# Group norm's scale and bias moved from the weights into the norm, the norm of later images moved to ScalarE, and a new order of the first loads and projections

## The chip, the cores and the metric

The kernel runs on one core of a Trainium2 chip. The metric is the device time of one execution in microseconds (us). Several executions were timed, and one was profiled.

## The reference, cut to what matters

Two layers on x of shape (8, 32, 32, 512), everything in float32. The change touches the first layer alone: a group norm with 32 groups of 16 channels, a projection to q, k and v, attention with 8 heads of 64, an output projection and a residual.

```python
xg = x.reshape(b, h * w, NUM_GROUPS, c // NUM_GROUPS)
mu = jnp.mean(xg, axis=(1, 3), keepdims=True)
var = jnp.var(xg, axis=(1, 3), keepdims=True)
xn = (xg - mu) * jax.lax.rsqrt(var + EPS)
x_norm = xn.reshape(b, h, w, c) * gn_scale + gn_bias
...
qkv = x_norm @ w_qkv + b_qkv
q, k, v = jnp.split(qkv, 3, axis=-1)
...
weight = jnp.einsum('bhld,bhsd->bhls', q * scale, k * scale)
weight = jax.nn.softmax(weight, axis=-1)
out = jnp.einsum('bhls,bhsd->bhld', weight, v)
...
out = out @ w_out + b_out
x = x_flat + out
```

`scale` is 1/8, so q and k together carry 1/64, which the kernel puts on q alone (`1.0 / HD`). The second layer is a deformable attention with a layer norm, a depthwise convolution, a bilinear gather, an attention over 256 sampled keys, and an MLP.

## The kernel before

An image has 1024 tokens, kept as 8 tiles of 128 tokens by 512 channels. The first layer works through the images one after the other, each in 32 steps of its main loop (line 728 on): 4 pairs of heads times 8 tiles of 128 queries. One such step calls `att.push` (line 749), which makes the scores of two heads on TensorE (`sc`, 128 x 1024 each), their row maxima on VectorE (`nmax`), the exponentials on ScalarE (`e`), and a 32 x 32 block transpose of them on VectorE (`sq`). After every second step the SP queue issues 16 DMAs (`moved`, line 204) that finish the transpose (`et`), and a few steps later TensorE multiplies `et` by the values (`av`). The scores of two heads fill the two `sc` buffers, so the scores of a step wait for the exponentials of the step before. There are two `e` buffers.

All other work of the layer is placed between these by hand. `at(place, step)` (line 347) puts a step on a list, and `run_due` issues what is due: between the exponentials and the transposes of step n all places under n + 0.8, after the transposes all under n + 1. `InOrder` (line 42) keeps every engine in this program order.

- `norm_steps` (line 440) loads and norms an image: `turn` (eight times) transposes a tile of x on TensorE into `xT` (channels on partitions, 512 tokens a block, two blocks an image, three buffers) with a copy by ScalarE, and asks POOL for the next tile of x; `two_tiles` takes statistics on VectorE; `gather`, `means` and `deviations` make the mean `mu` and the reciprocal deviation `rs` of every channel's group, with two small matmuls, and a power on POOL; `norm` applies them to the block, four VectorE instructions of 128 x 512 each. For an image after the first these stand in the previous image's loop, at the places in `norm_places` (line 718), counted from its start.
- `qkv_steps` (line 504) has six projections for one pair of heads: keys, queries and values for each of the two blocks (`rows` and `values`). For the first pair of the first image all six are issued before the loop (line 725, the place -1); for the first pair of a later image they stand at 26.3 to 31.3 of the image before (`pair_places[0]`).
- The group norm's scale is multiplied into `wqkv` in front of the loop (lines 419 to 421), as is q's 1/64. Its bias is multiplied by the weights with `add_cols` (line 415, 48 matmuls with one column) and added to `bqkv`. `add_row` (line 416) takes the values' part of that through `wout` and adds it to the row `bout`.
- In front of the loop POOL's queue loads four tiles of the first x (line 400, four buffers), and SP's queue loads the vectors, the three thirds of `wqkv`, `bout`, `wout` and two rows (lines 402 to 411). The last four tiles of x are asked for by `turn`, as buffers come free.

Of the kernel before, what the change touches and what calls it, by code (L numbers as in the profile page):

```python
# [9 lines left out]
F32 = mybir.dt.float32  # L10
I32 = mybir.dt.int32
AF = mybir.ActivationFunctionType
ALU = mybir.AluOpType
# [4 lines left out]
P = 128  # L18
B = 8
H = W = 32  # L20
S = H * W
C = 512
NC = C // P
NT = S // P
QB = 512
# [3 lines left out]
HD = 64  # L29
# [201 lines left out]
def attention_then_deformable_attention(  # L231
# [30 lines left out]
    nc = tc.nc  # L262
# [28 lines left out]
    def load_cols(pool, v, name):  # L291
        t = pool.tile([P, v.shape[0] // P], F32, tag=name, name=name)
        with nc.allow_non_contiguous_dma(reason="a vector onto partitions"):
            nc.sync.dma_start(t, v.rearrange("(c p) -> p c", p=P))
        return t
# [6 lines left out]
    def add_cols(dst, w, vec, on_scalar=False):  # L302

        n = dst.shape[1]
        ps = mm_tile()
        for o in range(n):
            for c in range(NC):
                nc.tensor.matmul(
                    ps[:, o : o + 1],
                    lhsT=w[:, c, ts(o, P)],  # L310
                    rhs=vec[:, c : c + 1],
                    start=(c == 0),
                    stop=(c == NC - 1),
                )
        if on_scalar:
            for o in range(n):
                col = dst[:, o : o + 1]
                nc.scalar.activation(col, ps[:, o : o + 1], AF.Identity, bias=col)
        else:
            nc.vector.tensor_tensor(dst, ps[:, 0:n], dst, ALU.add)  # L320
# [26 lines left out]
    def at(place, step):  # L347
        due.append((place, len(due), step))
# [37 lines left out]
    with ExitStack() as l0:  # L386
# [3 lines left out]
        nc = InOrder(tc)  # L390
# [2 lines left out]
        xs = {}  # L393

        def load_x(b, t):
            if b < B:
                xs[b, t] = work.tile([P, C], F32, tag="x", name="x", bufs=NX)
                nc.gpsimd.dma_start(xs[b, t], x_tok[b][ts(t, P), :])

        for t in range(NX):  # L400
            load_x(0, t)
        gsc = load_cols(wp, gn_scale, "gsc")
        gbi = load_cols(wp, gn_bias, "gbi")
        bqkv = load_cols(wp, b_qkv, "bqkv")
        wqkv = wp.tile([P, NC, 3 * C], F32, tag="wqkv", name="wqkv")
        for i in range(3):
            nc.sync.dma_start(wqkv[:, :, ts(i, C)], by_chunk(w_qkv)[:, :, ts(i, C)])
        bout = load_row(wp, b_out, "bout")
        wout = load_w(wp, w_out, "wout")
# [1 line left out]
        lnb_row = load_row(wp, ln_b, "lnb_row")  # L411

        add_cols(bqkv, wqkv, gbi)
        add_row(work, bout, wout, bqkv[:, 2 * NC : 3 * NC])


        for c in range(NC):
            nc.vector.tensor_scalar(wqkv[:, c, :], wqkv[:, c, :], gsc[:, c : c + 1], None, ALU.mult)  # L420
            nc.vector.tensor_scalar(wqkv[:, c, 0:C], wqkv[:, c, 0:C], 1.0 / HD, None, ALU.mult)
        nc.vector.tensor_scalar(bqkv[:, 0:NC], bqkv[:, 0:NC], 1.0 / HD, None, ALU.mult)


# [15 lines left out]
        def norm_steps(b, start, places):  # L440

            room = {}

            def turn(t):
                blk, i = divmod(t, NQT)
                if i == 0:
                    xTs[b, blk] = work.tile([P, NC, QB], F32, tag="xT", name="xT", bufs=NX_T)
                if t == 0:
                    room["stats"] = work.tile([P, NC, NT // 2, 6], F32, tag="stats", name="stats")
                ps = mm_tile()  # L450
                for c in range(NC):
                    nc.tensor.transpose(ps[:, ts(c, P)], xs[b, t][:, ts(c, P)], ident)
                nc.scalar.copy(xTs[b, blk][:, :, ts(i, P)], ps.rearrange("p (c q) -> p c q", q=P))
                load_x(b + (t + NX) // NT, (t + NX) % NT)

            def two_tiles(i):
                blk, half = divmod(i, NQT // 2)
                for c in range(NC):
                    nc.vector.bn_stats(
                        room["stats"][:, c, i, :], xTs[b, blk][:, c, ts(half, 2 * P)]  # L460
                    )


            def gather():
                mv = room["mv"] = work.tile([P, NC, 2], F32, tag="mv", name="mv")
                stats = room["stats"]
                for c in range(NC):
                    nc.vector.bn_aggr(mv[:, c, :], stats[:, c, :, :].rearrange("p s f -> p (s f)"))

            def means():  # L470
                mv = room["mv"]
                ps = mm_tile()
                nc.tensor.matmul(ps[:, 0:NC], lhsT=gmat, rhs=mv[:, :, 0], start=True, stop=True)
                mu = room["mu"] = work.tile([P, NC], F32, tag="mu", name="mu")
                nc.vector.tensor_copy(mu, ps[:, 0:NC])
                dev = room["dev"] = work.tile([P, NC], F32, tag="dev", name="dev")
                nc.vector.tensor_tensor(dev, mv[:, :, 0], mu, ALU.subtract)
                nc.vector.tensor_tensor(dev, dev, dev, ALU.mult)
                nc.vector.tensor_tensor(dev, dev, mv[:, :, 1], ALU.add)

            def deviations():
                ps = mm_tile()
                nc.tensor.matmul(ps[:, 0:NC], lhsT=gmat, rhs=room["dev"], start=True, stop=True)
                room["rs"] = work.tile([P, NC], F32, tag="rs", name="rs")
                rstd(room["rs"], ps[:, 0:NC], 1e-6)

            def norm(blk):
                xT, mu, rs = xTs[b, blk], room["mu"], room["rs"]
                for c in range(NC):
                    nc.vector.tensor_scalar(  # L490
                        xT[:, c, :], xT[:, c, :], mu[:, c : c + 1], rs[:, c : c + 1],
                        ALU.subtract, ALU.mult,
                    )

            steps = [
                *(lambda t=t: turn(t) for t in range(NT)),
                *(lambda i=i: two_tiles(i) for i in range(NT // 2)),
                gather, means, deviations,
                *(lambda blk=blk: norm(blk) for blk in range(NQB)),
            ]  # L500
            for place, what in zip(places, steps):
                at(start + place, what)

        def qkv_steps(b, hp, places):

            room = qkv[b, hp] = {}

            def rows(name, w0, bias, blk):
                if blk == 0:
                    room[name] = work.tile([P, S], F32, tag=name, name=name)  # L510
                xT = xTs[b, blk]
                ps = project(lambda c: wqkv[:, c, ds(w0, P)], lambda c: xT[:, c, :])
                out = room[name][:, ts(blk, QB)]
                if name == "k":
                    out = room[name].rearrange("p (s j q) -> p s j q", s=NSQ, q=SQ)
                    out, ps = out[:, :, ts(blk, NQT), :], att.by_blocks(ps)
                nc.scalar.activation(out, ps, AF.Identity, bias=bias)

            def values(t0):
                if t0 == 0:  # L520
                    room["v"] = work.tile([P, NT, P], F32, tag="v", name="v")
                xT = xTs[b, t0 // NQT]
                ps = mm_tile()
                for i in range(4):
                    for c in range(NC):
                        nc.tensor.matmul(
                            ps[:, ts(i, P)],
                            lhsT=xT[:, c, ts(i, P)],
                            rhs=wqkv[:, c, ds(2 * C + hp * P, P)],
                            start=(c == 0), stop=(c == NC - 1),  # L530
                        )
                nc.scalar.copy(room["v"][:, t0 : t0 + 4, :], ps.rearrange("p (t o) -> p t o", o=P))

            kb, qb = bqkv[:, NC + hp : NC + hp + 1], bqkv[:, hp : hp + 1]
            steps = [
                step
                for blk in range(NQB)
                for step in (
                    lambda blk=blk: rows("k", C + hp * P, kb, blk),
                    lambda blk=blk: rows("q", hp * P, qb, blk),  # L540
                    lambda blk=blk: values(blk * NQT),
                )
            ]
            for place, s in zip(places, steps):
                at(place, s)
# [73 lines left out]
        def first_conv(n):  # L619
# [98 lines left out]
        norm_places = [  # L718
            *(18.6, 19.6, 20.6, 21.6, 22.4, 22.5, 23.3, 23.4),
            *(20.85, 21.86, 22.86, 23.95),  # L720
            *(24.9, 24.96, 25.25, 25.85, 25.86),
        ]
        out_places = [0.3, 1.3, 4.3, 6.3, 7.3, 8.3, 10.3, 11.3]
        norm_steps(0, -100, norm_places)
        qkv_steps(0, 0, [-1] * 6)
        run_due(0)
        attT = {}
        for b in range(B):
# [487 lines left out]
```

## Time and profile before

| | us |
|---|---|
| median of 3 runs | 3833.03 |
| lowest and highest | 3826.36, 3833.45 |
| the profiled execution | 3831.76 |
| its span, first to last instruction | 3830.1 |
| TensorE busy in the span | 3609.5 (94%) |
| VectorE busy | 2831.4 (74%) |
| ScalarE busy | 1491.3 (39%) |
| GpSimd (POOL) busy | 754.9 (20%) |

The first layer takes the span's first 2100 us or so, the second the rest. Busy time on TensorE is not all work: a group of matmuls in which one waits for another engine still counts between its first and last record. In the profile PE is TensorE's matmul, DVE is VectorE, ACT is ScalarE and SPq the DMA issues of SyncE. L53 is the line of the helper that records every operation, so instructions are told apart by the tiles that they write and read, as in `sc<-k,q`. A float32 matmul of the program shows as two records. Three readings of the start:

```profile
x<-in_x_dram POOLq DMA_DIRECT2D x12, 256.0 KB, 3.4
wqkv<-in_L_conv_w_qkv_dram SPq DMA_DIRECT2D x3, 1024.0 KB, 10.0
...
bqkv<-in_L_conv_b_qkv_dram SPq DMA_DIRECT2D x1, 6.0 KB, 3.8
```

These are DMA issues of the first 60 us: how many, the size of each, and the median time from issue to landing.

### The profile page before, as it was taken

What the parts mean: (1) busy time and instruction counts of PE and PEld (TensorE: products, weight loads), DVE (VectorE), ACT (ScalarE), POOL (GpSimd) and SP (SyncE); (2) the same over time, 40 slices, a digit from 0 to 9 for tenths busy, and PEclk for the clock granted to TensorE, in tenths of its full rate; (3) what the DMA queues carried; (4) which work ended last, traced back from release to release, by engine and by line L of the source; (5) the groups of instructions that cost most, each with busy time, mean ns of one, the idle gap of its engine ahead of it and who ended that gap; (6) DMA issues with size and microseconds to landing.
All of it is one profiled execution on the core that took longest, in us unless ns stands there. A gap on an engine that the chain in (4) does not pass through costs nothing. (4 is left out here: it accounts for less than half of the span.)

```text
span 3830.1 us, 46258 instructions
## 1 busy us (share of the span) xinstructions
PE 3609.5 (94%) x16248; PEld 1889.5 (49%) x16248; DVE 2831.4 (74%) x4305; ACT 1491.3 (39%) x3162; POOL 754.9 (20%) x842
## 2 busy tenths in 40 slices
PE   7999999999999999999998877999999999999997
PEld 4454554545545545455454443454545445454543
DVE  3778677777776877767866659888888888888333
ACT  1443343433434434334354122343434444434443
POOL 1002103012030120210336300212121212121212
PEclk8999999999999999999999988999999999999999
DMA  2666566666665665665755501111111111111100
GB/s 92 163 162 181 157 157 187 162 166 167 163 188 155 164 179 160 172 165 149 206 139 148 171 25 53 47 57 54 56 55 56 55 55 56 55 52 34 61 23 30
DMA packets 235094, 438.23 MB, mean 114 GB/s; under 512 B 49296, under 2 KB 53392, under 8 KB 231920
## 3 DMA queue, kind: packets, MB, share of 16 engines
q1 hardware_dynamic: 211952, 362.04, 34.5%
q0 software_dynamic: 21760, 71.16, 5.9%
q8 instruction: 129, 2.11, 0.2%
q10 hardware_dynamic: 1152, 2.10, 0.1%
q14 instruction: 101, 0.83, 0.1%
HBM read 115.84 MB, written 50.86 MB: 44 GB/s over the span
## 5 line engine op out<-in xcount | busy, mean ns | idle before, releaser
L53 ACT ACTIVATE e<-sc,nmax 128x1024 f32<-128x1024 f32 (+1 forms) x1024 | 805.2, 799 | 951.9 <-DVE nmax L53 950.5
L53 DVE TENSOR_REDUCE nmax<-sc 128x1 f32<-128x1024 f32 (+1 forms) x640 | 753.2, 1218 | 471.6 <-PE sc L53 470.2
L53 DVE SCALAR_TENSOR_TENSOR o<-pad,dww,o 128x256 f32<-128x256 f32 x1344 | 721.8, 537 | 44.1
L53 DVE STREAM_TRANSPOSE sq<-e 128x1024 f32<-128x1024 f32 x512 | 608.6, 1226 | 50.5 <-ACT e L53 48.3
L53 PE MATMUL sc<-k,q 64*128 64x512 f32 x2048 | 537.4, 620 | 16.0 <-ACT e L53 9.1
L53 PE MATMUL av<-et,v 128*64 128x256 f32 x4096 | 502.2, 388 | 16.6 <-DMA et<-sq 9.7
L53 PE MATMUL mm<-xT,wqkv 128*128 128x512 f32 x1024 | 470.7, 603 | 2.1 <-DVE xT L53 2.1
L53 PEld LDWEIGHTS av<-et,v 128*64 128x64 f32 x4096 | 275.5, 137 | 321.0 <-issue 174.2
L53 POOL TENSOR_TENSOR mv<-mv,minus_half 128x1 f32<-128x1 f32 x128 | 74.3, 581 | 1401.8 <-DVE mv L53 1350.7
L53 PEld LDWEIGHTS sc<-k,q 64*128 64x128 f32 x2048 | 185.5, 187 | 285.9 <-issue 225.9
L53 PEld LDWEIGHTS mm<-xT,wqkv 128*128 128x128 f32 x1024 | 185.6, 190 | 225.4 <-issue 222.3
L53 ACT COPY et<-mm 128x512 f32<-128x512 f32 x256 | 141.1, 594 | 317.4 <-PE mm L53 316.8
L53 PE MATMUL mm<-wqkv,xT 128*128 128x128 f32 x2048 | 244.4, 278 | 0.0
L53 PE MATMUL mm<-wm,zT 128*128 128x512 f32 x512 | 241.0, 614 | 2.9 <-ACT zT L53 2.9
L53 PEld LDWEIGHTS mm<-wqkv,xT 128*128 128x128 f32 x2048 | 233.9, 192 | 19.6 <-issue 19.6
L53 PE MATMUL mm<-hat_h,wqq 128*128 128x512 f32 x512 | 236.7, 605 | 0.0
L53 PE MATMUL mm<-wo,attH 128*128 128x512 f32 x512 | 231.4, 595 | 4.3 <-DVE attH L53 4.3
L53 PE MATMUL mm<-wout,attT 128*128 128x512 f32 x512 | 233.7, 601 | 0.0
L53 ACT ACTIVATION_READ_ACCUMULATOR e<-sc,nmax 128x1 f32 x1024 | 209.1, 204 | 0.0
L53 PE MATMUL mm<-wq_r,hat 128*128 128x512 f32 x448 | 205.5, 602 | 0.2 <-ACT et L53 0.2
L53 PE MATMUL mm<-ident,e 128*128 128x128 f32 x1024 | 150.8, 291 | 27.0 <-DVE z L53 11.4
L53 POOL DMA_DIRECT2D x<-in_x_dram x64 | 36.2, 569 | 681.7 <-PE mm L53 681.3
(154 smaller groups left out, 3731.8 us busy)
## 6 DMA issues: line engine op xcount, KB each, us to landing
et<-sq SPq DMA_DIRECT2D x2048, 128.0 KB, 2.7
x<-in_x_dram POOLq DMA_DIRECT2D x64, 256.0 KB, 4.1
xr<-in_x_dram POOLq DMA_DIRECT2D x64, 256.0 KB, 4.1
hat_h<-hat_d SPq DMA_DIRECT2D x16, 1024.0 KB, 5.3
xr<-mid SPq DMA_DIRECT2D x64, 256.0 KB, 2.7
out_dram<-res POOLq DMA_DIRECT2D x64, 256.0 KB, 2.3
mid<-xr SPq DMA_DIRECT2D x56, 256.0 KB, 2.9
hat_d<-hat SPq DMA_DIRECT2D x56, 256.0 KB, 2.9
```

Of the source, the lines that this page charges most:

```text
L53: return self.tc.keep_in_program_order(op(*args, **kwargs))
```

## The change

The group norm's scale and bias are now applied together with the norm. `deviations` multiplies `rs` by the scale `gsc` and makes `nadd` = bias - mean x `rs` with three small VectorE instructions; `norm` then computes `xT` x `rs` + `nadd`. For the first image VectorE does it, as before; for the seven others ScalarE does, with `activation(Identity)` and two pointer operands. The weights are no longer scaled, `add_cols` in front of the loop is gone, and q's 1/64 goes into ScalarE's copy of q out of PSUM.

`add_row`, still needed for the values' bias, moves from in front of the loop to the place 5.4 of the first image. Of the first six projections three (keys of block 0, queries of block 0, keys of block 1) stay in front of the loop; the second queries move to 0.3, the two values steps to 1.3 and 2.3.

The first image's x is loaded at once: four tiles by POOL as before, four more by SP into `x2`, a buffer of the kind that `xT` uses, ahead of the vectors and weights. The keys' third of `wqkv` is loaded first. `turn` of the first image's first four tiles then asks for tiles of the second image. The second block's norm moves from 25.86 to 26.85, so that a keys projection (26.3) stands between the two halves of the norm.

```diff
         def load_x(b, t):
-            if b < B:
+            if b < B and (b, t) not in xs:
                 xs[b, t] = work.tile([P, C], F32, tag="x", name="x", bufs=NX)
                 nc.gpsimd.dma_start(xs[b, t], x_tok[b][ts(t, P), :])
 
+        x2 = work.tile([P, NC, QB], F32, tag="xT", name="x2", bufs=NX_T)
         for t in range(NX):
             load_x(0, t)
+            xs[0, NX + t] = x2[:, t, :]
+            nc.sync.dma_start(xs[0, NX + t], x_tok[0][ts(NX + t, P), :])
+        wqkv = wp.tile([P, NC, 3 * C], F32, tag="wqkv", name="wqkv")
         gsc = load_cols(wp, gn_scale, "gsc")
         gbi = load_cols(wp, gn_bias, "gbi")
         bqkv = load_cols(wp, b_qkv, "bqkv")
-        wqkv = wp.tile([P, NC, 3 * C], F32, tag="wqkv", name="wqkv")
-        for i in range(3):
+        for i in (1, 0, 2):
             nc.sync.dma_start(wqkv[:, :, ts(i, C)], by_chunk(w_qkv)[:, :, ts(i, C)])
...
-        add_cols(bqkv, wqkv, gbi)
-        add_row(work, bout, wout, bqkv[:, 2 * NC : 3 * NC])
-
-        for c in range(NC):
-            nc.vector.tensor_scalar(wqkv[:, c, :], wqkv[:, c, :], gsc[:, c : c + 1], None, ALU.mult)
-            nc.vector.tensor_scalar(wqkv[:, c, 0:C], wqkv[:, c, 0:C], 1.0 / HD, None, ALU.mult)
         nc.vector.tensor_scalar(bqkv[:, 0:NC], bqkv[:, 0:NC], 1.0 / HD, None, ALU.mult)
...
-                load_x(b + (t + NX) // NT, (t + NX) % NT)
+                if b > 0 or t < NX:
+                    load_x(b + (t + NX) // NT, (t + NX) % NT)
+                    if b == 0:
+                        load_x(1, t)
...
                 rstd(room["rs"], ps[:, 0:NC], 1e-6)
+                nc.vector.tensor_tensor(room["rs"], room["rs"], gsc, ALU.mult)
+                room["add"] = work.tile([P, NC], F32, tag="nadd", name="nadd")
+                nc.vector.tensor_tensor(room["add"], room["mu"], room["rs"], ALU.mult)
+                nc.vector.tensor_tensor(room["add"], gbi, room["add"], ALU.subtract)
...
             def norm(blk):
-                xT, mu, rs = xTs[b, blk], room["mu"], room["rs"]
+                xT, add, rs = xTs[b, blk], room["add"], room["rs"]
                 for c in range(NC):
-                    nc.vector.tensor_scalar(
-                        xT[:, c, :], xT[:, c, :], mu[:, c : c + 1], rs[:, c : c + 1],
-                        ALU.subtract, ALU.mult,
-                    )
+                    if b == 0:
+                        nc.vector.tensor_scalar(
+                            xT[:, c, :], xT[:, c, :], rs[:, c : c + 1], add[:, c : c + 1],
+                            ALU.mult, ALU.add,
+                        )
+                    else:
+                        nc.scalar.activation(
+                            xT[:, c, :], xT[:, c, :], AF.Identity,
+                            bias=add[:, c : c + 1], scale=rs[:, c : c + 1],
+                        )
...
-                nc.scalar.activation(out, ps, AF.Identity, bias=bias)
+                scale = 1.0 if name == "k" else 1.0 / HD
+                nc.scalar.activation(out, ps, AF.Identity, bias=bias, scale=scale)
...
-            *(24.9, 24.96, 25.25, 25.85, 25.86),
+            *(24.9, 24.96, 25.25, 25.85, 26.85),
...
         norm_steps(0, -100, norm_places)
-        qkv_steps(0, 0, [-1] * 6)
+        at(5.4, lambda: add_row(work, bout, wout, bqkv[:, 2 * NC : 3 * NC]))
+        qkv_steps(0, 0, (-1, -1, 1.3, -1, 0.3, 2.3))
```

## The prediction

> **What bounds the kernel now.** I call one `att.push` (one tile of 128 queries of one pair of heads) a unit; the first layer has 32 per image, 256 in all, and unit u of an image runs the steps placed from u to u+1. I read the page's slices first, then the timeline of the head, then busy time by stretch, then TensorE's timeline in the first units and around a norm.
>
> The page's slices (busy tenths, 96 us each):
>
> ```profile
> PE   7999999999999999999998877999999999999997
> ...
> PEclk8999999999999999999999988999999999999999
> ```
>
> TensorE is nearly full from slice 2 to 22, which is the first layer. Slice 1 is not, and there its clock is low too. The timeline of the head (start, length, engine, line, operation, what ended the idle time):
>
> ```profile
> 10.69 20.61 PE L53 MATMUL mm<-gbi,wqkv 128*128 128x1 f32 x96 [10.69 <-DMA wqkv<-in_L_conv_w_qkv_dram]
> ...
> 32.02 6.75 PE L53 MATMUL mm<-wout,rep_w 128*128 128x512 f32 x8 [0.72 <-DVE rep_w L53]
> ...
> 38.61 2.04 PE L53 MATMUL mm<-ident,x 128*128 128x128 f32 x16
> ...
> 45.14 5.32 DVE L53 BATCH_NORM_STATS2 stats<-xT 128x6 f32<-128x256 f32 x16
> ...
> 54.55 3.74 DVE L53 TENSOR_SCALAR xT<-xT,mu,rs 128x512 f32<-128x512 f32 x8 [1.16 <-POOL rs L53]
> ...
> 55.24 8.81 PE L53 MATMUL mm<-xT,wqkv 128*128 128x512 f32 x16 [2.06 <-DVE xT L53]
> ...
> 77.99 1.99 PE L53 MATMUL sc<-k,q 64*128 64x512 f32 x8
> ```
>
> Here the chain is serial: w_qkv lands, its product with the bias (20.61), the row product (6.75), transposes, statistics (held until 45.14 by the weight scaling on VectorE), norm, six projections, and the first scores at 77.99. All of that time is exposed.
>
> Busy time by stretch (window, length, PE, PEld, DVE, ACT, POOL, clock, DMA share, GB/s):
>
> ```profile
> 78.00:142.00 64.00, 57.73 (x249) 26.55 (x250) 48.64 (x44) 27.13 (x46) 0.00 (x0) 0.95 0.55 137
> ...
> 334.00:398.00 64.00, 63.35 (x296) 29.87 (x294) 49.77 (x63) 22.29 (x38) 22.95 (x24) 1.00 0.73 206
> ```
>
> The first units leave TensorE idle 6.3 of 64 us; later ones 0.7. The first units themselves:
>
> ```profile
> 82.53 4.25 PE L53 MATMUL sc<-k,q 64*128 64x512 f32 x8 [2.55 <-ACT e L53]
> 88.82 4.51 PE L53 MATMUL sc<-k,q 64*128 64x512 f32 x8 [2.04 <-ACT e L53]
> 93.26 3.70 PE L53 MATMUL mm<-xT,wqkv 128*128 128x512 f32 x8
> ...
> 107.03 3.11 PE L53 MATMUL sc<-k,q 64*128 64x512 f32 x8 [0.56 <-ACT e L53]
> 110.08 1.95 PE L53 MATMUL av<-et,v 128*64 128x256 f32 x16
> 111.95 3.70 PE L53 MATMUL mm<-xT,wqkv 128*128 128x512 f32 x8
> 115.58 1.99 PE L53 MATMUL sc<-k,q 64*128 64x512 f32 x8
> ```
>
> Scores that need 1.99 last 3.11 to 4.51: units 1 and 2 wait for the exponentials of the unit before (6.29 us from one to the next), so TensorE has room there. Around the norm of the second image (units 26 and 27 of the first):
>
> ```profile
> 261.57 5.61 DVE L53 TENSOR_SCALAR xT<-xT,mu,rs 128x512 f32<-128x512 f32 x8
> ...
> 266.27 3.70 PE L53 MATMUL mm<-xT,wqkv 128*128 128x512 f32 x8
> 267.10 2.34 DVE L53 TENSOR_REDUCE nmax<-sc 128x1 f32<-128x1024 f32 x2
> ...
> 269.90 2.87 PE L53 MATMUL sc<-k,q 64*128 64x512 f32 x8
> ```
>
> The maximum of unit 26 waits for eight norm instructions, its exponentials follow, and the scores of unit 27 stretch by 0.88. The same 2.87 to 2.9 stands at unit 27 of images 0 to 5, 2.2 at image 6.
>
> **What the Trainium skill says.** "TensorE: Matmul & The Clock Gate", section "What's actually happening": after idling the array runs at half clock until some 3.4 us of sustained work. The trace agrees: the first four projection records at 55.24 start 0.85 us apart, then 0.43. "Trainium Kernel Development and Optimization", section "Key Constraints": DMAs issued from SP and POOL share the same 16 engines, so issuing x from both saves issue time only; here the engines are full (share 1.03, 395 GB/s) from 7.5 to 10 us. "ScalarE: Activation LUTs", section "What ACT_TABLE_LOAD costs": an ACTIVATE of 512 columns with one pointer operand takes 280 + 0.833 x 512 = 707 ns, a second pointer adds 93, neighbours overlap by 93. The group rows:
>
> ```profile
> L53 ACT ACTIVATE q<-mm,bqkv 128x512 f32<-128x512 f32 x64 | 44.0, 687 | 135.7 <-PE mm L53 135.7
> ...
> L53 ACT ACTIVATE part_x<-rest_x,dww_x 128x256 f32<-128x256 f32 x96 | 49.7, 542 | 29.0 <-POOL o_x L53 29.0
> ```
>
> 687 against 707 agrees. The new norm instruction (two pointers) isn't in the trace: estimate 800 from the page, or 542 + 0.833 x 256 = 755 from the second row; spaced about 0.70. Bounds 0.6 and 0.9.
>
> **1. The head.** Gone: 20.61 and 6.75 on TensorE, the eight weight scalings (39.42 to 45.07), and the wait for weights ahead of all this. Now x starts. All of x is 2 MB: at 390 GB/s (seen from 7 us on) 5.4 us after a start at 2.5, so by 8. POOL's first tile lands at 4.88 as now. Transposes at half clock are 0.21 each (as at 45.3), 0.85 a tile: from 6.25 the second to eighth end near 12.2, copied by 12.9; last four statistics (0.33 each) end at 14.2. VectorE's first instruction now needs bqkv, issued behind four x tiles and two vectors, about 4.3 us, landing 8.5; 16 statistics from 8.8 end at 14.1. Both give 14.2. From the statistics' end to the first projection it was 55.24 - 50.46 = 4.78; three small VectorE operations at 0.195 are added: 14.2 + 4.78 + 0.59 = 19.6. w_qkv's key third (3 MB in all by then) lands near 11.5, the query third near 14: covered. Three projections: two took 55.24 to 63.89, 8.65 with the cold start; the third 3.41: end at 31.6. The key copy (0.69 and 0.2 to start) is now exposed: first scores at **32.5** instead of 77.99. Gain 45.5; bounds 40 and 48 (statistics ending 11.5 to 18, a clock window more or less).
>
> **2. What is moved into the units.** In time from the first scores; before, the scores of units 1 to 6 start at 4.5, 10.8, 18.9, 24.5, 29.0, 37.6. A row projection in the stream costs 3.63 (111.95 to 115.58), values 3.77, scores 1.92.
> Unit 0: scores, q (3.63): unit 1 at 5.55. Unit 1: scores, v: unit 2 at 11.25, exponentials ready. Unit 2: scores, v and the key step that stood there: 13.2 + 3.77 + 3.63 = 20.6, against 18.9: 1.7 late. So 9.3 of 11.0 us are hidden by the exponentials' chain. Units 3 to 5 keep 1.7.
> Unit 5 gets add_row besides av and q: four 512-column matmuls, 3.63; unit 6 starts at 42.9, 5.3 late. Its VectorE addition waits for these matmuls, and behind it in VectorE's order stand the transposes of unit 5 and the maximum of unit 6: 43.0 + 0.69 + 2.4 = 46.1 instead of 44.9. Unit 6 to 7 is bound by that chain, so 1.1 more: 6.4. Behind the transposes wait SP's 16 moves of units 4 and 5: 16 x 0.652 + 2.6 to land = 58.7, needed by av of unit 8 at 57.1: 1.5 late, but unit 9's scores then wait 1.1 less for exponentials. Sum at unit 10: **6.3 late**. Later units are full, and it stays. Bounds 4 (only the unhidden TensorE work) and 10 (both VectorE and SP lateness in full).
>
> **3. Norm on ScalarE, seven images.** Before the norm VectorE waits for POOL's power (ends 260.25) and does three small operations to 260.9; unit 25's transposes start 1.65 later and end at 263.3, before unit 26's maximum can start (264.5): covered; their moves are used in unit 28. ScalarE: behind the value copy (ends 263.2), four norms to about 266.1; the key projection starts at 266.27, covered by 0.2. The maximum of unit 26 is ready at 265.8, exponentials run 266.1 to 268.3 (before 268.4 to 270.6), so unit 27's scores no longer wait. Second half: behind the key copy, 270.7 to 273.5; its projection comes at 274.2: covered; unit 27's exponentials start at 273.5 (273.8 before). Gain 6 x 0.87 + 0.2 = **5.4**; bounds 0 (the wait stays) and, at 0.9 an instruction, a loss of 0.7 an image against it, still no less than 0.
>
> Scaling q in its copy is an immediate: nothing. The query and key thirds of w_qkv swapped, x2 in a buffer of xT (the same buffer three allocations later): nothing.
>
> **Sum.** 45.5 - 6.3 + 5.4 = 44.6. The profiled execution took 3831.76 (span 3830.1 and 1.7 around it): 3787.2. It lies 1.3 under the median 3833.03, against which the change stands: 3788.4, say 3788.
>
> **Rivals.**
> (a) SP's moves keep the lateness: each pair costs 13 us from transposes to landing, and in units 7 to 9 the chain leaves no room. Twice the give-back, 12.6: 3795. For it, av already waits for moves twice between 88 and 200 us, 1.6 in all; against, SP stands free 6.8 us before the moves of units 4 and 5.
> (b) The head starts later: eight x tiles, w_qkv and bqkv land together and bqkv gates all statistics, or the clock stays half through all three projections: 7 us, 3795. For it, bqkv took 3.8 us to land on emptier queues; against, x is ahead of the weights.
> (c) The norm does not do what it says: unit 27 still waits, now for ScalarE: 5.4 less, 3794.
> (d) Slower: ScalarE's norms stand ahead of the exponentials and the next projections. Cover is 3.1 for the first four (263.2 to 266.3) and 3.5 for the others, so at d each an image loses 8d - 6.6, and the 39.2 of the start are gone at 5.6 an image, d = 1.53. At 1.7 it is 7 x 7.0 = 49 and the time 3843. Against it, both nearest rows give half of that.
>
> **How the numbers follow.** Forecast 0.66, (a) 0.12, (b) 0.12, (c) 0.07, (d) 0.03. 0.2% of this time, 7.7 us, is about what can be told from no change. Only (d) is not faster: faster 0.96, same 0.01, slower 0.03. The range: bounds of the head 40 to 48, of the give-back 4 to 10, of the norm 0 to 5.4, not all at one end, and runs that themselves spread by 7: 3778 to 3801. (a), (b) and (c) lie in it one at a time.
>
> **What would show it.** First scores near 32.5; statistics' end near 14; unit 10 at 61.7 + 6.3 after the first scores; the scores of unit 27 at 1.99 in all images, image to image 249.9 instead of 250.7; norm instructions of 0.75 to 0.8. It is wrong if first scores come after 40, if av of units 8 to 12 waits long for moves, or if projections wait for ScalarE's xT.

## The result and the profile after

The changed kernel takes 3787.81 us (median of 4 runs, 3784.32 to 3793.69) against 3832.84 before (4 runs): a ratio of 0.9888, 95% interval 0.9871 to 0.9905, or 45.0 us less. The profiled execution took 3789.67, with a span of 3788.0, against 3830.1 before.

The page's slices of the changed kernel (95 us each): slice 1 is now nearly as full as the rest.

```profile
PE   8999999999999999999998787999999999999997
...
PEclk9999999999999999999999898999999999999999
```

The timeline of its head, in which the same steps are to be found as before, without the products with weights (a transpose shows as one record, four of them are a tile, so x24 are six tiles):

```profile
7.53 2.17 PE L53 MATMUL mm<-ident,x 128*128 128x128 f32 x8 [7.53 <-DMA x<-in_x_dram]
...
9.97 4.47 PE L53 MATMUL mm<-ident,x 128*128 128x128 f32 x24 [0.28 <-DMA x<-in_x_dram]
...
11.54 5.41 DVE L53 BATCH_NORM_STATS2 stats<-xT 128x6 f32<-128x256 f32 x16
...
22.26 12.90 PE L53 MATMUL mm<-xT,wqkv 128*128 128x512 f32 x24 [2.60 <-issue]
...
35.94 1.99 PE L53 MATMUL sc<-k,q 64*128 64x512 f32 x8 [0.78 <-ACT k L53]
```

The first scores start at 35.94 instead of 77.99, 42.05 earlier. Some of that is given back in the units that follow, and there the busy time by stretch shows something that was not foreseen (columns: window, length, PE, PEld, DVE, ACT, POOL, clock, DMA share, GB/s):

```profile
80.00:84.00 4.00, 2.40 (x20) 1.06 (x16) 3.85 (x4) 1.19 (x3) 0.00 (x0) 1.00 0.22 45
84.00:88.00 4.00, 3.93 (x8) 1.46 (x8) 3.56 (x5) 1.15 (x3) 0.00 (x0) 0.63 0.77 199
88.00:92.00 4.00, 4.00 (x18) 1.69 (x16) 3.40 (x4) 2.41 (x4) 0.00 (x0) 0.52 0.77 205
```

Behind the moved `add_row` TensorE waits, and its clock falls to half for some 7 us in the middle of the loop. The norm of the second image, on ScalarE:

```profile
229.51 2.93 ACT L53 ACTIVATE xT<-xT,nadd,rs 128x512 f32<-128x512 f32 x4
...
232.34 1.10 ACT L53 ACTIVATE e<-sc,nmax 128x1024 f32<-128x1024 f32 x1
232.72 3.70 PE L53 MATMUL mm<-xT,wqkv 128*128 128x512 f32 x8
...
236.35 1.99 PE L53 MATMUL sc<-k,q 64*128 64x512 f32 x8
```

The four instructions end before the projection that reads them, the exponentials follow at once, and the scores of unit 27 take 1.99 instead of 2.87. Where the time came from, in starts of scores read from the two traces:

| | before | after | earlier by |
|---|---|---|---|
| first scores | 77.99 | 35.94 | 42.05 |
| unit 10, after the first scores | 61.7 | 70.2 | -8.5 |
| first scores of the second image | 308.97 | 274.53 | 34.44 |
| first scores of the last image | 1812.96 | 1773.87 | 39.09 |
| from there to the end of the span | 2017.1 | 2014.1 | 3.0 |

Between the last two rows of starts lies the norm's part: 39.09 - 34.44 = 4.65 in six images, and 0.9 in the first. The 3.0 of the last row can't be put down to the change: in the thirteen profiles of this study that stretch took 2011.7 to 2027.3, among kernels that don't differ there. The times of one kernel spread by 9 us and more from run to run. So the experiments below are read by the starts of scores and not by a single time. Where nothing disturbs them, the steps from image to image repeat within 0.1 us; between the two profiles of the changed kernel (after_again is the second) the first scores differ by 0.7 us and those of the last image by 2.5.

### The profile page after: what moved, and what is told of

It reads as the page before. It is cut to its first block, busy times and chain, and to the rows that moved or that the text cites. A ratio compares the mean times of both kernels' runs of the same rounds, so it can differ in the third digit from the quotient of the medians.

```text
span 3788.0 us, 46075 instructions
## 1 busy us (share of the span) xinstructions
PE 3578.3 (94%) x16152; PEld 1868.9 (49%) x16152; DVE 2789.1 (74%) x4264; ACT 1529.3 (40%) x3218; POOL 750.6 (20%) x838
## 4 chain that ended last, share of the span: by engine, by line
PE 69%; DVE 20%; issue 6%; DMA 1%; ACT 1%; POOL 1%; SPq 0%; DVEq 0%; POOLq 0%; ACTq 0%
PE mm L53 42%; PE sc L53 15%; PE av L53 13%; DVE o L53 10%; DVE nmax L53 3%; DVE stats L53 1%; DVE sq L53 1%; DVE pad L53 1%; POOL mv L53 1%; ACT e L53 1%; DVE z L53 1%; DVE zn L53 1%; DVE attH L53 1%; DVE mv L53 1%; DMA row<-mid,ii 0%
## 5 line engine op out<-in xcount | busy, mean ns | idle before, releaser
L53 PE MATMUL sc<-k,q 64*128 64x512 f32 x2048 | 527.3, 618 | 13.5 <-ACT q L53 6.2
L53 PEld LDWEIGHTS mm<-hat_h,wqq 128*128 128x128 f32 x512 | 92.1, 189 | 143.0 <-issue 131.6
```

The costliest lines, as they stand in the source:

```text
L53: return self.tc.keep_in_program_order(op(*args, **kwargs))
```

## The experiments

All are the changed kernel with one edit. The table gives the first scores (A), the scores of unit 12 after them (B; 73.7 in the kernel before), the first scores of the last image (C), and the time (one run, except where more are named).

| run | A | B | C | time |
|---|---|---|---|---|
| the changed kernel, first profile | 35.94 | 82.2 | 1773.87 | 3787.81 (4 runs) |
| after_again | 35.28 | 80.4 | 1771.42 | 3788.43 (6 runs) |
| n_dve_86 | 35.19 | 82.1 | 1796.83 | 3812.64 |
| n_dve_split | 35.78 | 81.6 | 1776.87 | 3795.82 |
| n_act_86 | 36.19 | 82.2 | 1782.14 | 3804.29 |
| r_none | 36.13 | 76.2 | 1767.95 | 3782.68 |
| r_late_add | 36.39 | 80.8 | 1772.86 | 3786.88 |
| p_all_first | 45.16 | 79.1 | 1780.01 | 3795.12 |
| h_bq_late | 35.31 | 82.1 | 1773.09 | 3792.24 |
| h_swap | 35.34 | 82.2 | 1773.26 | 3793.01 |
| r_split | 35.18 | 77.1 | 1767.87 | 3785.48 (6 runs) |
| best | 35.84 | 77.1 | 1768.56 | 3784.10 (5 runs) |

**The norm: which engine, and in one piece or two.**

```diff
-                    if b == 0:
+                    if b < B:
                         nc.vector.tensor_scalar(
```
```diff
-            *(24.9, 24.96, 25.25, 25.85, 26.85),
+            *(24.9, 24.96, 25.25, 25.85, 25.86),
```

n_dve_86 has both edits, n_dve_split the first alone, n_act_86 the second alone.

> The changed kernel, with the norm of all images on VectorE and both halves together at 25.85 and 25.86, as before. Theory A (the eight VectorE instructions hold the row maximum of unit 26, that holds the exponentials and the scores of unit 27): the scores of unit 27 last about 2.9 again in images 0 to 5, image to image 250.7 instead of 249.9, and the first scores of the last image start 5 to 6 us later than the 1773.9 of the changed kernel. Rival B (the gain of the later images comes from something else, as the order of x or the missing scaling): 249.9 stays.

> The changed kernel, with the norm of all images on VectorE, but in two halves at 25.85 and 26.85. Theory A1 (it is enough to split the norm; ScalarE isn't needed): four instructions end near 265.5 on the clock of the kernel before, one us after the scores of unit 26, and the exponentials are in time: image to image 249.9, last image at 1774. Theory A2 (VectorE has no room for even half of it): image to image 250.3 to 250.7, last image 3 to 6 us later.

> The changed kernel, with the norm of later images on ScalarE, both halves together at 25.85 and 25.86. Theory A1 (the split is what counts): eight instructions of ScalarE at 0.7 take 5.6, the exponentials of unit 26 start near 268.8 on the clock of the kernel before (268.4 there), and the scores of unit 27 wait as before: image to image 250.7 to 251.2, last image 5 to 9 us later. Theory A2 (the engine counts): 249.9, last image at 1774.

From image to image the changed kernel takes 249.9 and the one before 250.7. n_dve_86 takes 252.2 to 255.6: theory A's direction, and in C four times its size. The timeline of that run tells why:

```profile
226.33 2.36 DVE L53 STREAM_TRANSPOSE sq<-e 128x1024 f32<-128x1024 f32 x2
...
228.62 5.60 DVE L53 TENSOR_SCALAR xT<-xT,rs,nadd 128x512 f32<-128x512 f32 x8
...
234.15 2.34 DVE L53 TENSOR_REDUCE nmax<-sc 128x1 f32<-128x1024 f32 x2
...
236.71 3.11 PE L53 MATMUL sc<-k,q 64*128 64x512 f32 x8 [1.16 <-ACT e L53]
```

The three small VectorE operations that the change adds wait for POOL's power, and the transposes wait behind them: these start 2.27 us after the second small matmul (224.06), against 0.78 in the kernel before, and with the norm in one piece on the same engine nothing covers that. TensorE now idles 1.16 before unit 27, and in images 1 and 3 (counted from 0) the clock falls behind it (the scores of unit 27 then last 4.8 and 4.0). So putting the scale and bias into the norm, by itself, makes the later images slower; moving the norm to ScalarE in two halves pays for it and for 0.8 an image more.

n_dve_split takes 250.4 and n_act_86 251.0 (1001.5 and 1004.1 us over four images, from the starts of images 2 and 6: 524.67 and 1526.18, 526.94 and 1531.08). So ScalarE in one piece isn't enough (its eight instructions take 5.75 and stand ahead of the exponentials), and the split on VectorE falls short by 0.5 an image. Why it does is seen in its two halves:

```profile
228.71 3.79 DVE L53 TENSOR_SCALAR xT<-xT,rs,nadd 128x512 f32<-128x512 f32 x4
228.95 2.81 POOL L53 TENSOR_TENSOR xr<-xr,bout 128x512 f32<-128x512 f32 x2 [1.92 <-DMA xr<-in_x_dram]
...
237.26 1.88 DVE L53 TENSOR_SCALAR xT<-xT,rs,nadd 128x512 f32<-128x512 f32 x4
```

In the first half two instructions last 1.49 instead of 0.54, those that run beside POOL's two additions of `bout` (228.95 to 231.76). The Trainium skill's "SBUF — State Buffer", section "Who interferes with whom", says that VectorE's `tensor_scalar` can take the port pair it shares with GpSimd, and that ScalarE waits for nobody. The traces agree: ScalarE's four take 2.93 beside POOL's additions and 2.92 without them.

In one image of n_dve_split (number 4, counted from 0) POOL's additions start 1.85 us after the norm does and miss its first half. There that half takes 1.87, the scores of unit 27 take 1.99, and the step to the next image is 249.9, all with the norm on VectorE. So the split on VectorE is enough where POOL's additions stay out of the way (theory A1), and ScalarE's merit here is that they don't slow it. The kernel before had the same trouble:

```profile
263.29 2.69 POOL L53 TENSOR_TENSOR xr<-xr,bout 128x512 f32<-128x512 f32 x2 [1.92 <-DMA xr<-in_x_dram]
```

These additions lie beside its norm of the second image, and two of the eight instructions take 1.49 there: 5.61 in all, against 3.74 for the first image, where POOL adds nothing. In image 6 only one is slowed (4.65 in all), and the scores of unit 27 take 2.19 instead of 2.87 to 2.90. So an estimate from these figures is that the kernel before would not have waited at unit 27 with POOL's additions elsewhere. A kernel with only that change was not run.

**The row product.** r_none drops the line `at(5.4, ... add_row ...)`. r_late_add keeps the matmuls at 5.4 and puts the addition to `bout` at 6.85.

> The changed kernel without add_row: the values' bias is left out of the row that is added behind the output projection. Theory C (the row product costs its 3.6 on TensorE and some 3.3 more, by the transposes and moves that wait behind its VectorE addition): from the first scores to unit 10 the time falls from 70.2 to 63.3, and the first scores of the last image start 6.9 earlier, at 1767. Rival D (it costs TensorE's 3.6 alone, and the rest of the 8.5 lost comes from the projections that were moved): 66.6, last image at 1770.3.

> The changed kernel, add_row's matmuls still at 5.4, its VectorE addition put off to 6.85, behind the transposes of unit 6. Theory C1 (the addition holds the transposes and the maximum; TensorE then idles over 2 us and its clock falls to half for some 7 us): the transposes of unit 5 end where they would without add_row, units 7 and 8 keep full clock, unit 10 starts 66 to 67 after the first scores instead of 70.2 (63.5 without add_row), the last image's first scores at 1770. Rival D1 (the lateness is TensorE's own work; the addition is harmless): unit 10 stays at 70, the last image at 1774.

Without it unit 10 comes at 63.5 and unit 12 at 76.2: against the first profile that is theory C's number, with `add_row` costing 6.0 of the lateness by unit 12, more than TensorE's 3.5. With the addition put off, TensorE keeps full clock, but unit 12 gains only 1.4 and C only 1.0: the full clock that C1 expected is there, the gain is not. A second profile of the changed kernel tells why:

> The changed kernel as it is, beside the two runs that follow. Every theory: 3784 to 3794, unit 12 at 82.2 after the first scores, the last image's first scores at 1773 to 1775.

```profile
83.41 3.11 PE L53 MATMUL sc<-k,q 64*128 64x512 f32 x8 [1.67 <-ACT e L53]
...
89.10 3.08 PE L53 MATMUL sc<-k,q 64*128 64x512 f32 x8
93.69 1.95 PE L53 MATMUL av<-et,v 128*64 128x256 f32 x16 [1.51 <-DMA et<-sq]
```

The same wait of 1.67 before unit 7 stands here, as in the first profile, but this time the clock doesn't fall (1.00 in all stretches from 76 to 96), and the products of unit 8 wait 1.51 for the moves. Unit 10 comes at 67.9 and unit 12 at 80.4. So the order of the instructions doesn't decide whether the clock falls: of seven profiles with `add_row` whole at 5.4 and the projections moved, five have the fall at unit 7, one behind unit 8, this one nowhere. It costs 1.8 at unit 12. At full clock `add_row` costs 4.4 at unit 10 and 4.2 at unit 12, which is TensorE's 3.5 and under 1 us more: theory C's reason, the work that waits behind the addition, has little part in it, and most of what went beyond rival D was the clock. Against this profile r_late_add gains nothing: it takes the wait of 1.51 away, and the products of unit 10 wait 1.08 for moves instead. So the addition's delay cost nothing in the end beyond the risk of the fall.

The traces narrow down what decides. In each of them the clock changes only at times that lie a multiple of 3.41 us apart (in the first profile at 16.8, 27.0, 85.1 and 91.9), and this grid begins elsewhere in every execution. In all seven profiles one stretch of the grid holds the whole wait before unit 7 (81.6 to 85.0 in the first, 80.2 to 83.6 in the second), and the profile has TensorE busy in it for 1.73 to 1.74 of 3.41 us; half clock follows five times, full clock twice. p_all_first, below, has the same wait of 1.67, but there it lies across two stretches (2.85 and 2.30 busy), and the clock stays. So it seems to depend on how the wait lies on the grid, with 1.74 of 3.41 near the limit. What tips the scale there stays open.

The cure is the place. r_split spreads the matmuls over two units that wait for exponentials.

```diff
-        at(5.4, lambda: add_row(work, bout, wout, bqkv[:, 2 * NC : 3 * NC]))
+        for place, cs in ((7.05, (0,)), (8.05, (1, 2, 3))):
+            at(place, lambda cs=cs: row_part(cs))
+        at(8.95, row_end)
```

> The changed kernel with add_row's four matmuls spread over two units whose scores wait for exponentials (one at 7.05, three at 8.05), and its VectorE addition at 8.95. Theory C (add_row costs 6.0 at 5.4, where TensorE is busy and VectorE must wait; where TensorE waits anyway it costs the part that doesn't fit, 0.9, and no fall of the clock): unit 12 at 77 to 78 after the first scores (76.2 without add_row, 82.2 at 5.4), the last image 4 to 5 earlier than the changed kernel, the time 4 to 5 less. Rival D (four matmuls cost their 3.4 to 3.6 wherever they stand): unit 12 at 79.8 or later.

```profile
85.03 1.13 PE L53 MATMUL mm<-wout,rep_w 128*128 128x512 f32 x2 [0.52 <-DVE rep_w L53]
86.09 1.99 PE L53 MATMUL sc<-k,q 64*128 64x512 f32 x8
...
89.88 2.84 PE L53 MATMUL mm<-wout,rep_w 128*128 128x512 f32 x6
```

Unit 12 at 77.1, 0.9 over r_none, as expected: the same four matmuls cost 0.9 here and 4.2 to 6.0 at 5.4. r_late_add also puts the addition off and also keeps full clock, and its unit 12 comes at 80.8, so the 3.7 between the two come from the matmuls' new places. Whether they had to be split for it as well as moved was not tried.

**The moved projections.** p_all_first puts all six back to the place -1.

> The changed kernel with all six first projections ahead of the first scores, as before, and add_row at 5.4. Theory E (the three moved projections are hidden but for some 1.7 us, by the exponentials' chain): first scores 9.6 to 10.5 later, at 45.5 to 46.5, unit 10 1.5 to 2 earlier after them, the last image's first scores 8 to 9 later, at 1782 to 1783. Rival F (TensorE has no room there and they are only shifted): unit 10 some 9 earlier after the first scores, the last image within 1.5 of 1774.

```profile
49.70 4.91 PE L53 MATMUL sc<-k,q 64*128 64x512 f32 x8 [2.55 <-ACT e L53]
56.09 4.42 PE L53 MATMUL sc<-k,q 64*128 64x512 f32 x8 [1.48 <-ACT e L53]
```

First scores 9.2 to 9.9 later than in the two profiles of the changed kernel, unit 6 1.6 earlier after them (41.0 against 42.6), C 6.1 to 8.6 later: theory E and not F. The clock doesn't fall at unit 7 in this run, so the second profile is the one to compare with, and against it first scores (9.9), unit 10 (1.5 earlier) and C (8.6) all lie in E's ranges. The scores of units 1 and 2 last 4.4 to 4.9 as in the kernel before, and in the changed kernel 2.0 to 2.1. In the kernel before the clock is 0.57 from 82 to 86 us: those units not only waited, they ran at half clock. With the projections moved between them neither happens.

**The head.** h_bq_late moves the scaling of q's bias behind the first norm; h_swap has also SP load tiles 0 to 3 and POOL tiles 4 to 7.

> The changed kernel, with the scaling of q's bias, VectorE's first instruction, moved behind the first image's norm, so that the statistics no longer wait for the bias to land (11.43). Theory G (the landing of x and the transposes at half clock set the end of the statistics): only 0.3 to 1 earlier, first scores at 35 to 35.6. Rival H (the bias gates the head): statistics start at 10.3 and end 1.2 earlier or more, first scores at 34.7 or before.

> The changed kernel with the bias scaling moved as in the run before, and the first four tiles of the first image loaded by SP, the last four by POOL (SP's tiles landed at 3.5 to 9.2, POOL's at 7.4 to 10.7). Theory G (the transposes start when the first tile lands; whoever issues x, all of it lands at 10.7): transposes start near 3.7 instead of 7.5, the last of them ends near 12 instead of 14.8, first scores 2.5 to 3.5 earlier, at 32.5 to 33.5. Rival (the array's half clock and the last landing keep it): less than 1 earlier.

Both first scores, 35.31 and 35.34, lie within what kernels with the same head show (35.2 to 36.4), so no gain was found: theory G for the bias, and for the swap the rival. In h_bq_late the statistics start at 10.79 instead of 11.54 and still end at 16.90 (16.94 in the first profile). The head of h_swap:

```profile
3.72 1.94 PE L53 MATMUL mm<-ident,x 128*128 128x128 f32 x8 [3.72 <-DMA x<-in_x_dram]
...
8.62 5.22 PE L53 MATMUL mm<-ident,x 128*128 128x128 f32 x24 [2.96 <-DMA x<-in_x_dram]
...
21.15 13.41 PE L53 MATMUL mm<-xT,wqkv 128*128 128x512 f32 x24 [2.59 <-issue]
```

The transposes start 3.8 earlier, but the third tile still lands only at 8.57, and the six from there on take some 0.85 each (half clock; in the kernel before the four from 38.61 on took 2.04). The statistics end at 15.93, 0.8 or more before those of the kernels with the old order (16.7 to 17.5), but the projections then take 13.41, at the long end of the 12.18 to 13.56 of kernels with the same three. In best the same head ends its statistics at 16.66.

**A version with the best of these.** best is r_split with h_swap's edits.

> The run before with the first four tiles of x loaded by SP and the bias scaling behind the norm (first scores 0.6 earlier when tried alone). Theory: the two add up, the last image's first scores 5 to 6 earlier than the changed kernel's, 1768 to 1769, the time 5 to 6 less than that of the changed kernel beside it, of which the spread of the runs (9) may hide most.

C is 2.9 to 5.3 earlier than in the two profiles of the changed kernel, so against the second it misses the 5 to 6 that were expected, and it is no earlier than r_split's: h_swap's edits add nothing. By times, measured beside each other: the changed kernel 0.9895 of before (0.9871 to 0.9920), r_split 0.9878 (0.9851 to 0.9905), best 0.9864 (0.9841 to 0.9887). The intervals overlap. That the first layer is shorter by 3.5 (r_split against after_again) is seen in the trace; that the whole kernel is faster than the changed one isn't shown.

## Why the prediction was right

Each of the three steps did what the forecast said, and nearly at its size. That the time came within 1 us of it is luck: up to the last image's first scores the gain is 39.1 to 41.5 (two profiles), not 44.6, and the rest of the 45.0 lies in the stretch behind and in the spread of the runs, which vary by more than that on their own.

- Step 1, the head: 45.5 predicted, 42.05 measured (42.71 in the second profile). What failed is the term for the landing of x, "5.4 us after a start at 2.5, so by 8". All of x landed at 10.66, POOL's first tile at 7.39 and not at 4.88, bqkv at 11.43 and not at 8.5: SP's tiles, issued at the same time, share the DMA engines, which were already 0.87 to 0.97 busy from 2.5 to 10 us while they moved 245 to 289 GB/s. The rate of 390 GB/s had been read from 7 us on; the trace of before had 146 GB/s from 2.5 to 5 us, and its first third of w_qkv, with x some 2 MB in all, had landed only at 10.55. That was the row to use. The statistics ended 2.7 late (16.95), and the three projections took 12.90 instead of 12.06, with more of them at half clock. The second part varies: in the second profile the clock came back at 25.6 instead of 27.0, and the projections took 12.18, so the landing is nearly the whole miss there. That transposes at half clock and bqkv's landing would both set the start was right, and h_bq_late shows that taking one away is not enough.
- Step 2, the give-back: 6.3 at unit 10, measured 6.2 in the profile without the fall of the clock, with its parts: unit 3 late by 1.6 (1.7 predicted), unit 6 at 42.6 (42.9), unit 7 at 48.1 (48.6), products of unit 8 waiting 1.51 for moves (1.5). It didn't quite stay there: by unit 12 it was 6.7. That the sum comes out is in part luck, since r_late_add, without the addition's delay and without that wait of 1.51, still has unit 10 at 67.6: one wait took the other's place. In the first profile the give-back was 8.5. The missing term is the fall of the clock before unit 8. The prediction reckoned with a falling clock in the head alone, and put units 1 and 2 of the kernel before (4.25 and 4.51) down to waiting, though half clock had its part in them.
- Step 3, the norm: 5.4 predicted, 5.5 measured. The instruction took 0.80, and 0.70 to 0.71 from start to start, as estimated (0.80 and 0.70). The three small VectorE operations were costed at nothing because VectorE had room before unit 26's maximum; n_dve_86 shows that this cover is not there when all eight norm instructions stay on VectorE. The prediction put the wait down to eight norm instructions and didn't see that POOL's additions made two of them nearly three times as long. It noted the shorter 2.2 at image 6, which shows this, and left it unexplained.
- Of the rivals, (c) and (d) did not come true. Of (a) there is the wait for moves in the second profile, at the size that the forecast itself gave it (1.51), and none in the first, where the clock fell. Of (b) about half came true: x and bqkv landed late together and the start was 2.8 to 3.4 late of its 7.

## What to carry to other kernels

Work that is moved behind a fill phase is cheap in units that wait for another engine and costs its full time, and what it makes late, in units that don't: list the waiting units and put it there in pieces. When an operation is taken over by another engine, look at what the change adds to the old engine too, and at the row that waits behind both. Before an operation is moved because it is slow in one place, look at what runs beside it there: the same instruction may be fast a few us later. For transfers at the start of a kernel take the landing times that the trace has for the same number of bytes, not the rate that it reaches later.

## What the runs showed of the hardware that was not expected

- A wait of 1.67 us of TensorE halved its clock for 6.8 us in one execution and not in another of the same code: unit 7's scores took 4.91 and 3.11. The clock changed only on a grid of 3.41 us, which lay differently in every execution.
- VectorE's `tensor_scalar` of 128 x 512 took 0.54 alone and 1.49 beside POOL's additions; ScalarE's ACTIVATE of the same tile 0.80 in both.
- One 256 KB tile issued by POOL at 1.4 us landed at 4.88 with SP's queue loading weights from 2.4 us on, and at 7.39 with SP's queue loading x from 0.8 us on.
